# A state-space layer rebuilt around units of one state and 1024 tokens, its products shared out over four engines

## The chip, the core and the metric

The kernel runs on one core of a Trainium2 chip. A core has a matrix engine (TensorE, PE in the profile; its weight loads are listed as PEld), a vector engine (VectorE, DVE), a scalar engine for activation functions (ScalarE, ACT), a general engine (GpSimd, POOL) and a sequencer that issues most transfers (SyncE, SP). Each engine works through its own list of instructions and waits on the others by semaphores. SBUF is the on-chip memory with 128 partitions; PSUM is the smaller memory that TensorE writes. The metric is the time of one execution on the device, in microseconds. All data is fp32.

## The reference

Two layers run one after the other on x of shape (4, 512, 32, 32), each with a group norm ahead of it and a residual around it. Layer 0 is a state-space (Mamba) block on 1024 tokens per batch, 1024 inner channels and 16 states; layer 1 is an attention block with two 3x3 convolutions. The change lies in layer 0:

```python
x = features.reshape(B, C, L).transpose(0, 2, 1)
xn = (x - mu) / jnp.sqrt(var + 1e-05) * ln_w + ln_b
xz = xn @ W_in
xm, z = (xz[..., :d_inner], xz[..., d_inner:])
xc = causal depthwise convolution of xm, 4 taps
xs = jax.nn.silu((xc + conv_b[None, :, None]).transpose(0, 2, 1))
proj = xs @ W_x
dt = jax.nn.softplus(proj[..., :dt_rank] @ W_dt + b_dt)
Bm = proj[..., dt_rank:dt_rank + D_STATE]
Cm = proj[..., dt_rank + D_STATE:]
A = -jnp.exp(A_log)
def step(h, inp):
    dt_t, B_t, C_t, x_t = inp
    dA = jnp.exp(dt_t[..., None] * A)
    h = dA * h + (dt_t * x_t)[..., None] * B_t[:, None, :]
    y = jnp.einsum('bds,bs->bd', h, C_t)
    return (h, y)
y = ys.transpose(1, 0, 2) + xs * D_param
y = y * jax.nn.silu(z)
out = y @ W_out
```

(The convolution's line is written in words.) For each of 4 batches, 1024 channels and 16 states there is thus a recurrence over 1024 tokens, with one product by B ahead of it, one by C behind it, and a sum over the 16 states.

## The kernel before

Channels lie on partitions, tokens along the row. A batch of 1024 tokens is cut into two halves of T = 512, so layer 0 runs over 8 half batches (index i, `b, h = divmod(i, NH)`). The 1024 inner channels are 8 blocks of 128 (index d), and each block has 16 states (s).

For each half batch, `phase1(i)` normalizes the tokens, multiplies them by W_in (L212), convolves on VectorE (L225, L227), applies Silu (L231), and computes the parameters `proj` (L237). The rows of B and C are stored to DRAM (`bcd`), and `load_bc` loads each of the 16 pairs back, spread over all 128 partitions (`bc`, 16 buffers). `delta(i, d)` makes dt by softplus, composed of Abs, Relu, Exp and Ln, and dt times x. Then for each state, at 512 tokens:

- ScalarE: `da` = Exp(A * dt), into PSUM (L340)
- GpSimd: `dbx` = (dt x) * B (L342)
- VectorE: `ht`, the scan h = da * h + dbx, into PSUM (L344); ScalarE copies its last column for the next half (L348)
- VectorE: `hc` = ht * C (L350)
- TensorE: `hc` is added into `py` by a matmul with the identity (L351)

After 16 states VectorE adds D x (L368), and GpSimd multiplies by the gate Silu(z) (L371), whose matmul is L308. `out_proj` (L264, L270) multiplies by W_out, adds x and stores the result `x1`, which layer 1 loads.

Python generators (`phase1`, `out_proj`, `delta`) are advanced a step at a time between the states, by `drain`, so that the work of the next half batch stands among the scans of this one. The order within each engine's list is then settled by a scheduler when the program is built, from these priorities and its own estimate of times; on the chip each engine takes its list as it stands. Buffers are counted per name (`bufs`): a tile waits until the tile that last used its slot has been read for the last time. Layer 1 transforms its convolution weights first (raw loads L406, sums on VectorE and GpSimd), then goes batch by batch: `norm`, `scores`, `conv3`, `attend`, `conv3`, `finish`. Both layers use `group_stats` (L86 to L100).

## Time and profile before

Three runs took 4080.11, 4087.10 and 4087.34 us; the median is 4087.1. The profiled execution took 4090.25 us, of which the profile's span is 4088.4.

| engine | busy us | share of the span | in layer 0 (0 to 2525.6) | in layer 1 |
|---|---|---|---|---|
| TensorE | 3091.6 | 76% | 1986.4 | 1105.3 |
| VectorE | 2964.2 | 73% | 2251.9 | 712.2 |
| ScalarE | 1704.4 | 42% | 1528.3 | 176.1 |
| GpSimd | 2239.1 | 55% | 1768.4 | 470.8 |

Layer 0 ends where SP issues layer 1's first load of raw weights, at 2525.6 us. Its scans run from 96.2 to 2500.5. Layer 1 has a stretch without large matmuls, from 2525.6 to 2839, in which the weights are transformed, and then four batches. The split columns are sums over windows of the trace.

How to read the lines below: a group's line gives source line, engine, operation, output and inputs with their shapes, the count, then the busy time and the mean length of one in ns, and after the second bar the idle time of the engine just before these instructions and what ended most of it. Instructions of one engine can overlap a little, so busy time divided by count may be shorter than the mean length. A timeline's line gives the start, the length, and how many instructions of one kind it puts together.

### The profile page before, as it was taken

What the parts mean: (1) busy time and instruction counts of PE and PEld (TensorE: products, weight loads), DVE (VectorE), ACT (ScalarE), POOL (GpSimd) and SP (SyncE); (2) the same over time, 40 slices, a digit from 0 to 9 for tenths busy, and PEclk for the clock granted to TensorE, in tenths of its full rate; (3) what the DMA queues carried; (4) which work ended last, traced back from release to release, by engine and by line L of the source; (5) the groups of instructions that cost most, each with busy time, mean ns of one, the idle gap of its engine ahead of it and who ended that gap; (6) DMA issues with size and microseconds to landing.
All of it is one profiled execution on the core that took longest, in us unless ns stands there. A gap on an engine that the chain in (4) does not pass through costs nothing.

```text
span 4088.4 us, 24690 instructions
## 1 busy us (share of the span) xinstructions
PE 3091.6 (76%) x6440; PEld 1214.0 (30%) x6440; DVE 2964.2 (73%) x3429; ACT 1704.4 (42%) x2771; POOL 2239.1 (55%) x1622
## 2 busy tenths in 40 slices
PE   6776887886887886887887875002987988988988
PEld 2222332322332322332322322000433333333334
DVE  5989999889999889999889996545434534535525
ACT  3675575675575675575676562101101200200200
POOL 1767767767767767768768783666112122221222
PEclk9998999998998998999999998555898898899799
DMA  4003003003003003002002003774626527428436
GB/s 149 36 1 93 18 4 93 21 1 93 17 5 93 21 1 93 16 6 82 18 4 83 21 0 99 235 266 155 236 85 233 204 85 266 173 94 282 151 111 242
DMA packets 165013, 397.36 MB, mean 97 GB/s; under 512 B 13768, under 2 KB 81608, under 8 KB 140296
## 3 DMA queue, kind: packets, MB, share of 16 engines
q1 hardware_dynamic: 150416, 371.82, 27.1%
q10 hardware_dynamic: 14456, 23.96, 1.7%
q8 instruction: 51, 0.84, 0.1%
q14 instruction: 90, 0.74, 0.1%
HBM read 328.11 MB, written 67.63 MB: 97 GB/s over the span
## 4 chain that ended last, share of the span: by engine, by line
PE 28%; DVE 10%; POOL 9%; issue 7%; DMA 3%; ACT 2%; POOLq 0%; DVEq 0%; SPq 0%; ACTq 0%
PE m_b L613 9%; PE m_o L613 8%; PE pat L661 5%; DVE ht L344 3%; PE psc L519 2%; DVE hc L350 2%; PE py L351 2%; POOL dbx L342 2%; DMA x1t<-x 1%; PE po L264 1%; ACT da L340 1%; DVE xs L227 1%; ACT L340 1%; POOL dt L298 0%; POOL u L297 0%
## 5 line engine op out<-in xcount | busy, mean ns | idle before, releaser
L342 POOL TENSOR_TENSOR dbx<-dtx,bc 128x512 f32<-128x512 f32 x1024 | 1323.5, 1307 | 553.3 <-DVE ht L344 538.8
L351 PE MATMUL py<-hc,ident 128*128 128x512 f32 x2048 | 1126.4, 664 | 449.6 <-DVE hc L350 445.0
L340 ACT ACTIVATE da<-dt,a_sb 128x512 f32<-128x512 f32 x1024 | 699.7, 691 | 418.7 <-DVE ht L344 414.7
L351 PEld LDWEIGHTS py<-hc,ident 128*128 128x128 f32 x2048 | 365.5, 200 | 1169.4 <-DVE hc L350 1015.2
L350 DVE TENSOR_TENSOR hc<-ht,bc 128x512 f32<-128x512 f32 x1024 | 666.7, 677 | 49.2 <-ACT state L348 29.1
L344 DVE TENSOR_TENSOR_SCAN ht<-da,state,dbx 128x512 f32<-128x512 f32 x512 | 636.5, 1277 | 46.5 <-POOL dbx L342 24.1
L344 DVE TENSOR_TENSOR_SCAN ht<-da,dbx 128x512 f32<-128x512 f32 x512 | 607.8, 1218 | 65.1 <-POOL dbx L342 30.0
L613 PE MATMUL m_o<-uw_o,v_o 128*128 128x512 f32 x768 | 341.6, 607 | 56.1 <-DVE v_o L600 56.1
L613 PE MATMUL m_b<-uw_b,v_b 128*128 128x512 f32 x768 | 357.6, 624 | 5.7 <-DVE v_b L600 5.7
L264 PE MATMUL po<-xs,wpr_sb 128*128 128x512 f32 x512 | 255.7, 623 | 16.7 <-POOL xs L371 16.7
L308 PE MATMUL pz<-xt,win_sb 128*128 128x512 f32 x512 | 255.3, 613 | 14.2 <-ACT state L348 10.4
L212 PE MATMUL pxm<-xt,win_sb 128*128 128x512 f32 x512 | 248.7, 611 | 11.1 <-DVE xt L203 7.0
L98 PE MATMUL pv_l<-gdev_l,gm_sb 128*128 128x1 f32 (+1 forms) x40 | 10.9, 342 | 309.8 <-DVE gdev_l L96 309.8
L348 ACT COPY state<-ht 128x1 f32<-128x1 f32 x512 | 78.7, 157 | 379.4 <-DVE ht L344 377.6
L340 ACT ACT_TABLE_LOAD x179 | 229.7, 1283 | 3.1
L613 PEld LDWEIGHTS m_o<-uw_o,v_o 128*128 128x128 f32 x768 | 149.0, 195 | 248.4 <-issue 184.8
L661 PE MATMUL pat<-y_b,st 128*128 128x512 f32 x512 | 220.4, 592 | 0.0
L613 PEld LDWEIGHTS m_b<-uw_b,v_b 128*128 128x128 f32 x768 | 149.4, 198 | 210.8 <-issue 199.9
L227 DVE SCALAR_TENSOR_TENSOR xs<-xm,cw_sb,xs 128x512 f32<-128x512 f32 x192 | 176.0, 917 | 1.8
L667 DVE SCALAR_TENSOR_TENSOR xg<-pat,rz,xg 128x512 f32<-128x512 f32 x32 | 24.1, 752 | 195.9 <-PE pat L661 195.9
L621 ACT ACTIVATE e_o<-m_o 128x512 f32<-128x512 f32 x24 | 14.3, 597 | 336.8 <-PE m_o L613 336.8
L264 PEld LDWEIGHTS po<-xs,wpr_sb 128*128 128x128 f32 x512 | 102.2, 201 | 150.1 <-issue 123.4
(208 smaller groups left out, 3540.2 us busy)
## 6 DMA issues: line engine op xcount, KB each, us to landing
uw_b<-u_b SPq DMA_DIRECT2D x96, 1024.0 KB, 4.8
uw_o<-u_o SPq DMA_DIRECT2D x96, 1024.0 KB, 4.8
bc<-bcd SPq DMA_DIRECT2D x128, 512.0 KB, 5.4
u_b<-o_b SPq DMA_DIRECT2D x16, 768.0 KB, 5.3
u_o<-o_o SPq DMA_DIRECT2D x16, 768.0 KB, 3.8
raw_b<-in_w_bottom_dram SPq DMA_DIRECT2D x8, 1152.0 KB, 9.2
raw_o<-in_w_out_dram SPq DMA_DIRECT2D x8, 1152.0 KB, 9.2
xt<-in_x_dram SPq DMA_DIRECT2D x8, 1024.0 KB, 5.3
```

Of the source, the lines that this page charges most:

```text
L212: nc.tensor.matmul(pxm, win_sb[:, c, d * P : (d + 1) * P], t[:, c, :], start=(c == 0), stop=(c == NCC - 1),)
L227: nc.vector.scalar_tensor_tensor(u, xm[:, k : k + T], cw_sb[:, 4 * d + k : 4 * d + k + 1], u, ALU.mult, ALU.add,)
L264: nc.tensor.matmul(po, wpr_sb[:, d, c * P : (c + 1) * P], xs[i][d], start=(d == 0), stop=(d == NDC - 1),)
L308: nc.tensor.matmul(pz, win_sb[:, c, DI + d * P : DI + (d + 1) * P], xt[i][:, c, :], start=(c == 0), stop=(c == NCC - 1),)
L340: nc.scalar.activation(da, dt, AF.Exp, scale=a_sb[:, k : k + 1])
L342: nc.gpsimd.tensor_mul(dbx, dtx, bc[:, 0, :])
L344: nc.vector.tensor_tensor_scan(ht, da, dbx, 0.0 if h == 0 else state[:, k : k + 1], ALU.mult, ALU.add)
L350: nc.vector.tensor_mul(hc, ht, bc[:, 1, :])
L351: nc.tensor.matmul(py, ident, hc, start=(s == 0), stop=(s == NS - 1))
L519: nc.tensor.matmul(pt, top[:, m * P : (m + 1) * P], center[:, h * T : (h + 1) * T], start=True, stop=True,)
L613: nc.tensor.matmul(m[q], v[:, q, k, c, :], w[:, c, :], start=(c == 0), stop=(c == NCC - 1 and not extra),)
L661: nc.tensor.matmul(pt, st[m][:, 2 * P * j + h : 2 * P * (j + 1) : 2], xb[m // 2][:, m % 2, :], start=(m == 0), stop=(m == NMC - 1),)
```

## The change

Layer 0 is rewritten; layer 1 differs only in `group_stats`, which takes 1/sqrt by Ln and Exp on ScalarE (`rsqrt`) instead of Sqrt and a reciprocal on VectorE.

- A unit is now one state of one channel block over all 1024 tokens of a batch: 512 units in place of 1024 half units; the state is no longer carried over, and `state` is gone.
- The B product is made in two ways. For the nine states in `B_ON_ACT`, dt x is transposed once per block (`dtxt`, tokens on partitions), ScalarE scales eight 128x128 pieces by B's column (`sc`), and TensorE transposes them back into PSUM (`u`). For the other seven, B is loaded from DRAM over all partitions (`bbc`) and GpSimd multiplies (`dbx`); there `u` holds the Exp.
- The C product is on GpSimd for twelve states and on VectorE for the four in `C_ON_DVE`. C is loaded for every unit (`cbc`, three buffers) instead of once per half batch.
- The sum over states is made by transposes of `hc` that add up in PSUM (`y`, tokens on partitions); at the end of a block the sum is copied and transposed back (`gate`).
- W_in is scaled by ln_w, stored to DRAM (`wind`) and loaded in slices; ln_b goes into biases. The convolution reads PSUM, its first tap on ScalarE. Softplus is one activation. The gates go to DRAM (`szd`) and back, as do the gated outputs (`gd`), and W_out is loaded in slices with one buffer.
- `background` says what of the next batch stands beside which block: norms (n), convolution blocks (digits), gates (z), parameters (p).

The diff, its added lines cut to the core:

```diff
+    def rsqrt(out, var):
+        nc.scalar.activation(out, var, AF.Ln, bias=eps)
+        nc.scalar.activation(out, out, AF.Exp, scale=-0.5)
...
-        nc.scalar.activation(rstd, pv[:, :n], AF.Sqrt, bias=eps)
-        nc.vector.reciprocal(rstd, rstd)
+        rsqrt(rstd, pv[:, :n])
...
-        bp = l0.enter_context(tc.tile_pool(name="l0bc", bufs=NS))
         mmp = l0.enter_context(tc.tile_pool(name="l0mm", bufs=2, space=PSUM))
-        yp = l0.enter_context(tc.tile_pool(name="l0y", bufs=2, space=PSUM))
-        ap = l0.enter_context(tc.tile_pool(name="l0a", bufs=2, space=PSUM))
-        hp = l0.enter_context(tc.tile_pool(name="l0h", bufs=2, space=PSUM))
+        yp = l0.enter_context(tc.tile_pool(name="l0y", bufs=1, space=PSUM))
+        up = l0.enter_context(tc.tile_pool(name="l0u", bufs=2, space=PSUM))
+        NT = L // P
+        NK = T // P
+        halves = [slice(h * T, (h + 1) * T) for h in range(NH)]
+        B_ON_ACT = (0, 2, 4, 6, 8, 9, 11, 13, 15)
+        C_ON_DVE = (1, 5, 10, 14)
...
+        wind = dram.tile([2 * NDC, P, NCC, P], F32, tag="wind", name="wind")
...
+                nc.vector.tensor_scalar_mul(ws[c], ws[c], lnw_sb[:, c : c + 1])
+                nc.sync.dma_start(
+                    wind[k * NDC : (k + 1) * NDC, :, c, :].rearrange("k p n -> p k n"),
+                    ws[c].rearrange("p (k n) -> p k n", n=P),
+                )
...
+        def conv1(b, d):
+            w = load_win(b, d)
+            u = sp.tile([P, L], F32, tag="xs", name=f"xs_{b}_{d}", bufs=10)
+            hist = spool.tile([P, 3], F32, tag="hist", name=f"hist_{b}_{d}")
+            cw = [cw_sb[:, 4 * d + 3 - k : 4 * d + 4 - k] for k in range(4)]
+            for h, hs in enumerate(halves):
+                p = mmp.tile([P, T], F32, tag="mm", name=f"pxm_{b}_{d}_{h}")
+                for c in range(NCC):
+                    nc.tensor.matmul(
+                        p, w[:, c, :], xt[b][:, c, hs], start=(c == 0), stop=(c == NCC - 1)
+                    )
+                uh = u[:, hs]
+                nc.scalar.activation(uh, p, AF.Copy, scale=cw[0])
                 if h == 0:
+                    nc.scalar.copy(hist, p[:, T - 3 :])
                 for k in range(1, 4):
                     nc.vector.scalar_tensor_tensor(
+                        uh[:, k:], p[:, : T - k], cw[k], uh[:, k:], ALU.mult, ALU.add
+                    )
...
                 yield
+            nc.scalar.activation(u, u, AF.Silu, bias=cb_sb[:, d : d + 1])
+            xs[b, d] = u
...
+        def gates(b, d):
+            w = load_win(b, NDC + d)
+            sz = sp.tile([P, L], F32, tag="sz", name=f"sz_{b}_{d}", bufs=1)
+            for h, hs in enumerate(halves):
+                p = mmp.tile([P, T], F32, tag="mm", name=f"pz_{b}_{d}_{h}")
+                for c in range(NCC):
+                    nc.tensor.matmul(
+                        p, w[:, c, :], xt[b][:, c, hs], start=(c == 0), stop=(c == NCC - 1)
+                    )
+                nc.scalar.activation(
+                    sz[:, hs], p, AF.Silu, bias=bx[:, NDC + d : NDC + d + 1]
+                )
+                yield
+            nc.sync.dma_start(szd[b][d], sz)
...
+        def params(b):
+            p0 = b % 2 * NP
+            for h, hs in enumerate(halves):
+                pp = mmp.tile([P, T], F32, tag="mm", name=f"pp_{b}_{h}")
                 for d in range(NDC):
                     nc.tensor.matmul(
+                        pp[p0 : p0 + NP, :], wx_sb[:, d, :], xs[b, d][:, hs],
                         start=(d == 0), stop=(d == NDC - 1),
                     )
+                nc.scalar.copy(proj[p0 : p0 + NP, hs], pp[p0 : p0 + NP, :])
                 yield
+            nc.sync.dma_start(bcd[b], proj[p0 + RK : p0 + NP, :])
...
+            nc.vector.tensor_copy(bt_sb[b % 2], pt[:, :, RK : RK + NS])
...
+        def delta(b, d):
+            rows = slice(b % 2 * NP, b % 2 * NP + RK)
+            dt = sp.tile([P, L], F32, tag="dt", name=f"dt_{b}_{d}")
+            for h, hs in enumerate(halves):
+                pd = mmp.tile([P, T], F32, tag="mm", name=f"pd_{b}_{d}_{h}")
+                nc.tensor.matmul(
+                    pd, wdt_sb[rows, d * P : (d + 1) * P], proj[rows, hs],
+                    start=True, stop=True,
+                )
+                nc.scalar.activation(dt[:, hs], pd, AF.Softplus, bias=bdt_sb[:, d : d + 1])
+            yield
+            dtx = sp.tile([P, L], F32, tag="dtx", name=f"dtx_{b}_{d}")
+            nc.gpsimd.tensor_mul(dtx, dt, xs[b, d])
+            yield
+            dtxt = sp.tile([P, NT, P], F32, tag="dtxt", name=f"dtxt_{b}_{d}")
+            for h in range(NH):
+                pt = mmp.tile([P, NK, P], F32, tag="mm", name=f"pdt_{b}_{d}_{h}")
+                for k in range(NK):
+                    at = h * NK + k
+                    nc.tensor.transpose(pt[:, k, :], dtx[:, at * P : (at + 1) * P], ident)
+                nc.scalar.copy(dtxt[:, h * NK : (h + 1) * NK, :], pt)
+            dts[b, d] = dt, dtx, dtxt
...
+        def unit(b, d, s, y):
+            dt, dtx, dtxt = dts[b, d]
+            name = f"{b}_{d}_{s}"
+            c_bc = sp.tile([P, L], F32, tag="cbc", name=f"cbc_{name}", bufs=3)
+            nc.sync.dma_start(c_bc, bcd[b][NS + s].partition_broadcast(P))
+            u = up.tile([P, L], F32, tag="u", name=f"u_{name}")
+            scale = a_sb[:, d * NS + s : d * NS + s + 1]
+            if s in B_ON_ACT:
+                sc = sp.tile([P, NT, P], F32, tag="sc", name=f"sc_{name}")
+                for k in range(NT):
+                    nc.scalar.activation(
+                        sc[:, k, :], dtxt[:, k, :], AF.Copy,
+                        scale=bt_sb[b % 2][:, k, s : s + 1],
+                    )
+                    nc.tensor.transpose(u[:, k * P : (k + 1) * P], sc[:, k, :], ident)
+                da = sp.tile([P, L], F32, tag="da", name=f"da_{name}")
+                nc.scalar.activation(da, dt, AF.Exp, scale=scale)
+                dbx = u
+            else:
+                b_bc = sp.tile([P, L], F32, tag="bbc", name=f"bbc_{name}")
+                nc.sync.dma_start(b_bc, bcd[b][s].partition_broadcast(P))
+                dbx = sp.tile([P, L], F32, tag="dbx", name=f"dbx_{name}")
+                nc.gpsimd.tensor_mul(dbx, dtx, b_bc)
+                da = u
+                nc.scalar.activation(da, dt, AF.Exp, scale=scale)
+            hc = sp.tile([P, L], F32, tag="hc", name=f"hc_{name}", bufs=3)
+            if s in C_ON_DVE:
+                nc.vector.tensor_tensor_scan(u, da, dbx, 0.0, ALU.mult, ALU.add)
+                nc.vector.tensor_mul(hc, u, c_bc)
+            else:
+                ht = sp.tile([P, L], F32, tag="ht", name=f"ht_{name}")
+                nc.vector.tensor_tensor_scan(ht, da, dbx, 0.0, ALU.mult, ALU.add)
+                nc.gpsimd.tensor_mul(hc, ht, c_bc)
+            for k in range(NT):
+                nc.tensor.matmul(
+                    y[k // NK][:, k % NK, :], hc[:, k * P : (k + 1) * P], ident,
+                    start=(s == 0 and k % NK == 0), stop=(s == NS - 1 and k % NK == NK - 1),
+                    is_transpose=True, skip_group_check=True,
+                )
+        def gate(b, d, y):
+            sz = sp.tile([P, L], F32, tag="szl", name=f"szl_{b}_{d}", bufs=1)
+            nc.sync.dma_start(sz, szd[b][d])
+            yt = sp.tile([P, NT, P], F32, tag="yt", name=f"yt_{b}_{d}", bufs=1)
+            g = sp.tile([P, L], F32, tag="g", name=f"g_{b}_{d}", bufs=1)
+            u = xs.pop((b, d))
+            for h, hs in enumerate(halves):
+                nc.scalar.copy(yt[:, h * NK : (h + 1) * NK, :], y[h])
+            for h, hs in enumerate(halves):
+                p = mmp.tile([P, T], F32, tag="mm", name=f"pyb_{b}_{d}_{h}")
+                for k in range(NK):
+                    nc.tensor.transpose(p[:, k * P : (k + 1) * P], yt[:, h * NK + k, :], ident)
+                nc.vector.scalar_tensor_tensor(
+                    p, u[:, hs], dp_sb[:, d : d + 1], p, ALU.mult, ALU.add
+                )
+                nc.vector.tensor_mul(g[:, hs], p, sz[:, hs])
+            nc.sync.dma_start(gd[b][:, d, :], g)
+            del dts[b, d]
...
+        def out_proj(b):
+            src = x[b].rearrange("(c p) h w -> p c (h w)", p=P)
+            wsrc = w_proj.rearrange("(d p) n -> p d n", p=P)
+            for h, hs in enumerate(halves):
+                gt = sp.tile([P, NDC, T], F32, tag="gt", name=f"gt_{b}_{h}", bufs=1)
+                nc.sync.dma_start(gt, gd[b][:, :, hs])
+                for c in range(NCC):
+                    w = sp.tile([P, NDC, P], F32, tag="wpr", name=f"wpr_{b}_{h}_{c}", bufs=1)
+                    nc.sync.dma_start(w, wsrc[:, :, c * P : (c + 1) * P])
+                    res = sp.tile([P, T], F32, tag="res", name=f"res_{b}_{h}_{c}", bufs=3)
+                    nc.sync.dma_start(res, src[:, c, hs])
+                    po = mmp.tile([P, T], F32, tag="mm", name=f"po_{b}_{h}_{c}")
+                    for d in range(NDC):
+                        nc.tensor.matmul(
+                            po, w[:, d, :], gt[:, d, :], start=(d == 0), stop=(d == NDC - 1)
+                        )
+                        if d == NDC // 2 - 1:
+                            yield
+                    nc.vector.tensor_add(res, res, po)
+                    nc.sync.dma_start(x1[b][h][c * P : (c + 1) * P, :], res)
...
+        def background(b, d):
+            n = b + 1
+            if b == 0 and d < 2:
+                for k in range(4 * d, 4 * d + 4):
+                    yield from gates(b, k)
+                return
+            if n == B:
+                return
+            plan = (
+                {2: "n0", 3: "123", 4: "45z", 5: "6zz", 6: "7pz", 7: "zzzz"}
+                if b == 0
+                else {0: "n", 1: "01", 2: "23", 3: "4z", 4: "5zz", 5: "6zz", 6: "7pz", 7: "zz"}
             )
+            for what in plan.get(d, ""):
+                if what == "n":
+                    load_x(n)
+                    yield from norms(n)
+                elif what == "z":
+                    yield from gates(n, zs.pop(0))
+                elif what == "p":
+                    yield from params(n)
+                else:
+                    yield from conv1(n, int(what))
...
+        drain(norms(0))
+        for d in range(NDC):
+            drain(conv1(0, d))
+        drain(params(0))
+        drain(delta(0, 0))
+        opr = iter(())
+        for b in range(B):
+            zs = list(range(NDC))
             for d in range(NDC):
+                bg = background(b, d)
+                if d + 1 < NDC:
+                    ahead = delta(b, d + 1)
+                elif b + 1 < B:
+                    ahead = delta(b + 1, 0)
+                else:
+                    ahead = iter(())
+                y = [
+                    yp.tile([P, NK, P], F32, tag=f"y{h}", name=f"y_{b}_{d}_{h}")
+                    for h in range(NH)
+                ]
                 for s in range(NS):
+                    unit(b, d, s, y)
+                    drain(bg, 1)
+                    if d < 4 and s % 4 == 1:
+                        drain(opr, 1)
+                    if s >= 10 and s % 2 == 0:
                         drain(ahead, 1)
+                drain(bg)
                 drain(ahead)
+                gate(b, d, y)
+            opr = out_proj(b)
+        drain(opr)
```

## The prediction

> **What bounds the kernel now.** The windows come first, cut at the first scan (94.2), the end of the last scan's work (2500.5), the first load of layer 1 (2525.6) and layer 1's first large matmuls (2839). Columns: stretch, length, busy time of each engine, granted clock, DMA share, GB/s.
>
> ```profile
> 0.00:94.20 94.20, 57.73 (x117) 22.67 (x118) 47.12 (x77) 25.59 (x45) 11.14 (x22) 0.94 0.41 128
> 94.20:2500.50 2406.30, 1909.81 (x3830) 698.28 (x3828) 2201.22 (x2558) 1502.75 (x2437) 1755.97 (x1392) 0.95 0.12 36
> 2500.50:2525.60 25.10, 18.83 (x40) 7.70 (x38) 3.58 (x6) 0.00 (x0) 1.26 (x1) 0.93 0.22 73
> ```
>
> Layer 0 lasts 2525.6 us, and in its 2406.3 us of scans VectorE is busy for 2201.2, 91%. The groups say with what, and the waits that it hardly ever stands still:
>
> ```profile
> L342 POOL TENSOR_TENSOR dbx<-dtx,bc 128x512 f32<-128x512 f32 x1024 | 1323.5, 1307 | 553.3 <-DVE ht L344 538.8
> L351 PE MATMUL py<-hc,ident 128*128 128x512 f32 x2048 | 1126.4, 664 | 449.6 <-DVE hc L350 445.0
> L350 DVE TENSOR_TENSOR hc<-ht,bc 128x512 f32<-128x512 f32 x1024 | 666.7, 677 | 49.2 <-ACT state L348 29.1
> L344 DVE TENSOR_TENSOR_SCAN ht<-da,state,dbx 128x512 f32<-128x512 f32 x512 | 636.5, 1277 | 46.5 <-POOL dbx L342 24.1
> L344 DVE TENSOR_TENSOR_SCAN ht<-da,dbx 128x512 f32<-128x512 f32 x512 | 607.8, 1218 | 65.1 <-POOL dbx L342 30.0
> ```
>
> The last number before the arrow is idle time ahead of the group: 160.8 us for all scans and products together, while GpSimd, TensorE and ScalarE (414.7 at L340) each wait 400 us and more for VectorE. The others run ahead of the scan; nothing after it returns to it soon. So VectorE's work is the time: 1911 us of scans and C products.
>
> **Prices.** The timeline shows what instructions back to back take (start, length, engine, line, count):
>
> ```profile
> 399.71 2.41 DVE L344 TENSOR_TENSOR_SCAN ht<-da,state,dbx 128x512 f32<-128x512 f32 x2
> 406.57 1.26 DVE L350 TENSOR_TENSOR hc<-ht,bc 128x512 f32<-128x512 f32 x2
> 401.03 2.48 POOL L342 TENSOR_TENSOR dbx<-dtx,bc 128x512 f32<-128x512 f32 x2 [3.02 <-DVE ht L344]
> 2842.37 1.24 ACT L510 ACTIVATE top<-pt,bt_sb 64x128 f32<-64x128 f32 x4
> 4074.86 1.21 PE L685 MATMUL po<-ident,y_o 128*128 128x128 f32 x8 [1.28 <-POOL y_o L634]
> 65.95 3.70 PE L212 MATMUL pxm<-xt,win_sb 128*128 128x512 f32 x8 [0.23 <-ACT hist L223]
> ```
>
> Over 1024 tokens I take: scan 2.4, product 1.2 on VectorE and 2.5 on GpSimd, Exp 1.1 (1135 ns at L533); eight 128x128 transposes 1.1 (L685, 1.21 with the first one's latency); a 512-column matmul 0.92 (3.70 for four); a table load 1.28. A 128x128 ScalarE copy with its own scale has no row. From below it is a quarter of the 0.58 between two 512 copies, 0.15; from above the 128x128 Exp at L143, 0.31; four 128-wide copies follow each other by 0.26 at L510. I take 0.22, eight in 1.8.
>
> **The change by engine sums.** There are 512 units (4 batches, 8 channel blocks, 16 states). VectorE: 512 scans x 2.4 = 1229, 128 products x 1.2 = 154, convolution 192 x 0.62 plus corrections 140, gate 64 x 1.3 = 83, norms and output adds 90: about 1700, where it had 2250 in layer 0. GpSimd: (224 + 384) x 2.5 = 1520 plus 48 others = 1640. ScalarE: 2304 copies x 0.22 = 507, 512 Exp = 563, other 300, some 260 table loads = 333: 1700 (1540 to 1910 by the bounds). TensorE: 4096 + 2304 + 512 transposes x 0.137 = 950, and 830 matmuls x 0.92 and more = 900: 1850. By sums alone layer 0 would fall. The page "TensorE: Matmul & The Clock Gate" of the Trainium skill, section "Part 4: PE-mode transpose", speaks against it: a 128x128 transpose took about 275 ns inside a kernel there; the row above has 1.21 us for eight. By that figure the 6900 transposes would be an estimated 1900 us, not 950, and the forecast some 700 us longer; the row decides here.
>
> **What the sums leave out: who waits for whom.** In which order the instructions stand on each engine in the changed program is known before it runs. TensorE's list goes: part of u(s+2), y(s), y(s+1), rest of u(s+2), with matmuls of the next batch between them. y(s) is the transposes that add state s into the sum; it waits for the C product, mostly GpSimd's, which waits for scan s. u(s+2) is needed by scan s+2, and its slot (two in PSUM) is free only after scan s. So the scan now waits for a chain that starts at the scan before it: C product 2.5 (5 when two stand in a row), y 1.1, last u 0.3. Nothing in the trace of before has such a return. I walked the four lists by hand with the prices above and 0.1 per hand-over, first batch 3, block 5, which has no side work. Scan 1 starts at 0. Scan 2 runs 3.6 to 6.0; GpSimd's product 2 to 8.6; y2 to 9.8; the eighth transpose of u4 to 10.1; scan 4 starts at 10.2 where scan 3 ended at 8.4: 1.8 lost. In the same way scan 6 loses 1.8 (behind y4), scan 8 4.3 (y6 and y7; product 7 follows product 6 on GpSimd), scan 11 5.2 (its u stands among transposes of the next block's dt*x, which GpSimd makes after products 8, 9 and one B product), scan 13 4.3 (y11, y12), scan 15 2.4 (y13), the next scan 0 4.2 (y15). That is 24.0 lost on 16 x 2.4 + 4 x 1.2 + gate 2.6 = 45.8 of work: 69.8 us for the group; the next scan 1 waits for y15, the copy of y, its transposes back and the gate.
>
> Side work makes it longer, since matmuls stand ahead of u on TensorE. In batch 1, block 2 (two convolutions, two output blocks, 32 matmuls) u2 comes after 12 matmuls and y1, and scan 2 starts at 14.9 instead of 3.6; I reach 92, with 56 of VectorE work. Batch 1, block 5 (24 matmuls) gives 85; batch 3, block 1 (16) gives 73. The slope from 70 is 0.2 to 0.7 us a matmul; I take 0.6. Convolutions, gates, output, norms and parameters put 192 + 256 + 192 + 48 + 48 = 736 matmuls beside the 32 groups. Groups: 32 x 70 + 736 x 0.6 = 2240 + 440 = 2680, 84 each.
>
> **The ends of layer 0.** Nothing covers them. Before the first scan everything is now done for 1024 tokens: eight convolution blocks at 7.4 (two times 3.70) instead of 4.2, +26; the parameter matmuls +7; the second half's norm (3.7 + 2.5 + 3.8, Ln and Exp with two table loads 3.8) +14; GpSimd's four products 10 instead of 5; more tables, weights scaled and sent through DRAM, transposes, +15. From 96 this makes 165 (140 to 190). After the last scan: gate 9; g stored and 2 MB of it loaded twice, 11 each (2 MB landed in 11.4 at start); eight blocks of 7.4 on TensorE, each behind a 512 KB slice of w_proj in its only buffer (5.4 to landing by the bc loads), the first slice loaded early, 97: 128 (95 to 150) where 25 was. SP issues layer 1's first load behind all of these stores, so layer 1 moves with them. The new group_stats takes Ln and Exp for a root and a reciprocal: 16 times in layer 1 up to 2.8 more, some hidden by loads: +15 (0 to 45). Conv edges, folded bias and ln weights are in the walked lists.
>
> **Sum.** 165 + 2680 + 128 = 2973 against 2525.6: +447; layer 1 +15. The profiled execution took 4090.25 (span 4088.4), 3.1 above the median of 4087.1: 4090 + 462 = 4552, told as 4550. Break-even is (2525.6 - 293 - 15) / 32 = 69.3 us a group: even the group without side work lies there.
>
> **Bounds.** GpSimd's 1024 product is 2.35 by L634 (the shortest 128x1024 sum) and 2.84 by L640; eight transposes are 1.0 or, by the last twelve of L685 in 2.79, 1.9. That makes the bare group 68 to 79; with a slope of 0.2 to 0.8 the groups are 2320 to 3120, and the time, with the ends' bounds, 4130 to 5070. SP's new loads (736 broadcasts of 512 KB, 377 MB, 140 GB/s over the groups) stand in three and two buffers; the 16 such loads around 380 us ran at 300 GB/s and landed in 5.4, a product uses its own three units (12 us) after its slot frees, so I cost them at nothing, up to 5 us a group where szl or gd stands before them.
>
> **Rivals.** (a) The waits matter less than walked: the scheduler's lists meet another rhythm, u is done early, and a group follows the engine sums plus some 10 us, 60 to 64 in the mean. Then 293 + 32 x 62 = 2277, and the time is 3860. For it: four nearly equal sums of 50 to 58 a group. Against: y before u in the lists, and no slack in two slots. It decides where a group's mean falls under 69.3. (b) ScalarE or the loads add to the chain: table loads (15 of them, 19 us, in the block with four gates) and copies at 0.31 put it beyond 66 in gate and norm blocks, or C broadcasts come late: 8 to 12 more a group, 4870. For it: Silu, Exp and Softplus alternate in the list; against: ScalarE's Exp and copies mostly stand ahead of their use in my walks.
>
> **How the numbers follow.** Forecast 0.65, (b) 0.20, (a) 0.13, and 0.02 around no change. The slower cases reach from 4130 to 5070; I cut both outer edges and take 4220 to 4870, which leaves out (a) and the top of (b). Faster 0.12, within 0.2% 0.01 (about what a measurement of this kernel can tell), slower 0.87.
>
> **What would show it.** Right: first scan near 165; VectorE near 60% in layer 0; groups of 70 to 75 us in batch 3 and 85 to 95 before; the largest waits TensorE's y for GpSimd's C product and VectorE's scan for TensorE's u; layer 1's first load near 2970; layer 1 itself nearly unchanged. Wrong: VectorE, GpSimd or TensorE above 85% in the scans, a group mean under 70, or scans that wait for loads.

## The result and the profile after

The changed kernel takes 4685.3 us (median of four runs, 4682.98 to 4688.07); the kernel before, on the same chip, 4086.8 us (four runs, 4080.11 to 4087.34). The ratio is 1.147, with a 95% interval of 1.145 to 1.149: 15% slower. The forecast was 4550 us, in a range of 4220 to 4870. The profiled execution took 4686.39 us, with a span of 4684.6.

The windows of the changed kernel, cut at its first scan, the end of its last scan, and layer 1's first load (columns as before: stretch, length, busy time of TensorE, weight loads, VectorE, ScalarE, GpSimd, granted clock, DMA share, GB/s):

```profile
0.00:167.30 167.30, 129.40 (x359) 69.15 (x360) 56.74 (x127) 55.33 (x81) 14.62 (x12) 0.96 0.33 104
167.30:2974.07 2806.77, 1978.51 (x8506) 1344.53 (x8504) 1564.12 (x1106) 1800.37 (x3459) 1513.50 (x649) 0.80 0.53 176
2974.07:3111.88 137.81, 80.28 (x144) 34.28 (x144) 8.35 (x13) 2.43 (x4) 2.34 (x1) 0.70 0.28 88
3111.88:4684.50 1572.62, 1106.68 (x2456) 486.56 (x2456) 707.53 (x772) 208.87 (x328) 471.69 (x208) 0.80 0.54 188
```

The second line is the case. In 2806.8 us of scans VectorE is busy for 1564.1 (56%; it was 91%), TensorE for 70%, ScalarE for 64%, GpSimd for 54%. VectorE has less to do, no engine took its place as the bound, and the stretch became 400 us longer. Where the engines stand still is in the groups (busy time and mean length in ns of one, then idle time ahead and what ended it):

```profile
L379 POOL TENSOR_TENSOR hc<-ht,cbc 128x1024 f32<-128x1024 f32 x384 | 898.6, 2350 | 1130.4 <-DVE ht L378 1082.5 <-issue 42.2 <-PE u L361 3.9
L381 PE MATMUL y<-ident,hc 128*128 128x128 f32 x4096 | 771.8, 352 | 646.3 <-POOL hc L379 615.9 <-DVE hc L375 29.7
L357 ACT ACTIVATE sc<-dtxt,bt_sb 128x128 f32<-128x128 f32 x2304 | 712.3, 389 | 38.1 <-PE u L361 38.0
L378 DVE TENSOR_TENSOR_SCAN ht<-da,u 128x1024 f32<-128x1024 f32 x288 | 656.1, 2284 | 1027.8 <-PE u L361 861.8 <-ACT sc L357 74.1 <-POOL dbx L369 49.4
L361 PE MATMUL u<-ident,sc 128*128 128x128 f32 x2304 | 436.7, 322 | 161.2 <-DVE ht L378 90.6 <-ACT sc L357 66.8 <-ACT da L363 3.7
```

The waits form a ring. GpSimd's C product waits 1082.5 us for the scan, TensorE's y waits 615.9 for the C product, and the scan waits 861.8 for TensorE's u. Before, the idle time on the scans' lines was 46.5 and 65.1. No engine of the ring is busy for more than some 70% of the stretch; each waits for another. The link that closes the ring is the order of TensorE's list, which these sums don't show as a wait: u itself waits only 161.2 us, because it stands behind y. Scan 8 of the block below shows it: GpSimd's two C products end at 2797.80, y runs from 2797.86, the last two transposes of u follow at 2799.62, and the scan starts at 2800.39.

The same can be seen state by state. VectorE's timeline for batch 3, block 5, which has no work beside it (start, length, idle before and its releaser; only the gates at both ends and the scans that waited are shown):

```profile
2769.02 1.39 DVE L400 SCALAR_TENSOR_TENSOR pyb<-xs,dp_sb,pyb 128x512 f32<-128x512 f32 x2
...
2777.39 2.29 DVE L378 TENSOR_TENSOR_SCAN ht<-da,u 128x1024 f32<-128x1024 f32 x1 [2.33 <-PE u L361]
2784.18 2.29 DVE L378 TENSOR_TENSOR_SCAN ht<-da,u 128x1024 f32<-128x1024 f32 x1 [2.32 <-PE u L361]
2790.76 2.29 DVE L378 TENSOR_TENSOR_SCAN ht<-da,u 128x1024 f32<-128x1024 f32 x1 [0.85 <-PE u L361]
2800.39 4.46 DVE L378 TENSOR_TENSOR_SCAN ht<-da,u 128x1024 f32<-128x1024 f32 x2 [5.16 <-PE u L361]
2813.11 2.29 DVE L378 TENSOR_TENSOR_SCAN ht<-da,u 128x1024 f32<-128x1024 f32 x1 [4.81 <-ACT sc L357]
2821.96 2.29 DVE L378 TENSOR_TENSOR_SCAN ht<-da,u 128x1024 f32<-128x1024 f32 x1 [4.38 <-PE u L361]
2831.97 2.29 DVE L378 TENSOR_TENSOR_SCAN ht<-da,u 128x1024 f32<-128x1024 f32 x1 [4.27 <-PE u L361]
2839.04 2.29 DVE L378 TENSOR_TENSOR_SCAN ht<-da,u 128x1024 f32<-128x1024 f32 x1 [4.79 <-PE u L361]
2841.24 1.39 DVE L400 SCALAR_TENSOR_TENSOR pyb<-xs,dp_sb,pyb 128x512 f32<-128x512 f32 x2
```

From gate to gate the block takes 72.2 us. The scans shown are those of states 2, 4, 6, 8, 11, 13, 15 and of the next state 0: all the scans whose B product goes through TensorE, except scan 9, which follows scan 8 at once. Their idle times add up to 28.9. (Scan 11, the line with ScalarE's sc, started just after the last transpose of its u had ended, at 2812.97; the first five of the eight had run at 2810.81, and the other three stood among transposes of the next block's dt times x, which GpSimd finished at 2812.05.) The scans whose B product is GpSimd's (1, 3, 5, 7, 10, 12, 14) are not late.

Block times by batch, from the first L400 instruction of one block's end to that of the next, averaged over a batch's eight blocks: 93.4, 92.7, 91.7 and 73.8 us. Batch 3's blocks 4 to 7, with nothing beside them, took 72.5, 72.2, 73.7 and 64.6.

### The profile page after: what moved, and what is told of

It is laid out like the page before. It is cut to its first block, busy times and chain, and to the rows that moved or that the text cites. A ratio compares the mean times of both kernels' runs of the same rounds, so it can differ in the third digit from the quotient of the medians.

```text
span 4684.6 us, 34360 instructions
## 1 busy us (share of the span) xinstructions
PE 3294.9 (70%) x11464; PEld 1934.5 (41%) x11464; DVE 2336.7 (50%) x2018; ACT 2067.0 (44%) x3871; POOL 2002.1 (43%) x870
## 5 line engine op out<-in xcount | busy, mean ns | idle before, releaser
L379 POOL TENSOR_TENSOR hc<-ht,cbc 128x1024 f32<-128x1024 f32 x384 | 898.6, 2350 | 1130.4 <-DVE ht L378 1082.5
L381 PE MATMUL y<-ident,hc 128*128 128x128 f32 x4096 | 771.8, 352 | 646.3 <-POOL hc L379 615.9
L378 DVE TENSOR_TENSOR_SCAN ht<-da,u 128x1024 f32<-128x1024 f32 x288 | 656.1, 2284 | 1027.8 <-PE u L361 861.8
L381 PEld LDWEIGHTS y<-ident,hc 128*128 128x128 f32 x4096 | 636.2, 183 | 866.2 <-POOL hc L379 774.8
L357 ACT ACTIVATE sc<-dtxt,bt_sb 128x128 f32<-128x128 f32 x2304 | 712.3, 389 | 38.1 <-PE u L361 38.0
L369 POOL TENSOR_TENSOR dbx<-dtx,bbc 128x1024 f32<-128x1024 f32 x224 | 527.5, 2357 | 161.0 <-DMA bbc<-bcd 65.8
L361 PE MATMUL u<-ident,sc 128*128 128x128 f32 x2304 | 436.7, 322 | 161.2 <-DVE ht L378 90.6
L361 PEld LDWEIGHTS u<-ident,sc 128*128 128x128 f32 x2304 | 340.0, 170 | 276.9 <-ACT sc L357 172.3
L729 PE MATMUL m_b<-uw_b,v_b 128*128 128x512 f32 x768 | 358.7, 626 | 10.4 <-DVE v_b L716 10.4
L363 ACT ACTIVATE da<-dt,a_sb 128x1024 f32<-128x1024 f32 x288 | 328.2, 1140 | 0.9
L374 DVE TENSOR_TENSOR_SCAN u<-u,dbx 128x1024 f32<-128x1024 f32 x128 | 292.0, 2281 | 25.7 <-POOL dbx L369 14.3
```

The costliest lines, as they stand in the source:

```text
L357: nc.scalar.activation(sc[:, k, :], dtxt[:, k, :], AF.Copy, scale=bt_sb[b % 2][:, k, s : s + 1],)
L361: nc.tensor.transpose(u[:, k * P : (k + 1) * P], sc[:, k, :], ident)
L363: nc.scalar.activation(da, dt, AF.Exp, scale=scale)
L369: nc.gpsimd.tensor_mul(dbx, dtx, b_bc)
L374: nc.vector.tensor_tensor_scan(u, da, dbx, 0.0, ALU.mult, ALU.add)
L378: nc.vector.tensor_tensor_scan(ht, da, dbx, 0.0, ALU.mult, ALU.add)
```

## The experiments

All runs are of the changed kernel with the edit whose core is shown, unless it is said otherwise; a time without a range is that of a single run; line numbers in a run's profile shift with its edit. Their block times are taken as above.

### y behind u: same work, another order on TensorE

```diff
-                    unit(b, d, s, y)
+                    held.append((s, unit(b, d, s, y)))   # returns hc
+                    if len(held) > 2:
+                        with tc.issue_after(last_u[0].ins):
+                            add_y(y, *held.pop(0))        # the eight transposes of L381
```

> The changed kernel with one difference: TensorE's list. The transposes that add state s into the sum (y) are given out two units later and stand behind the last transpose of u(s+2), so that u(s+2) no longer stands behind y(s), which waits for the C product of s. All engines do the same work, hc keeps three buffers, u two. Theory (the return chain scan, C product, y, u, scan through TensorE's list costs the time): the walk of batch 3, block 5 by the new list loses some 14 us instead of 24, most of it at u11 and at the block's end; 58 to 62 us where 72 were measured, groups of the other batches near 72 instead of 92, so layer 0 near 2520 and the time 4000 to 4250. Rival (ScalarE's copies, table loads, or the slower TensorE set the time, the order of y only fills what is left): the engines' work is the same, the groups stay within 4 us of 88, time above 4550. Rival (loads of C come late): the same, above 4550.

It took 4232.75 us (4226.05 to 4243.08; ratio to before 1.035, 1.033 to 1.036): 452.6 less than the changed kernel, three quarters of the loss, for an order alone. Batch means are 78.0, 77.0, 76.5 and 64.7 us, the block looked at 60.6: the block as walked, the other batches some 5 us over what was expected. Its windows' second line, and the group of its scans:

```profile
167.33:2532.89 2365.56, 1830.41 (x8506) 1234.88 (x8504) 1590.44 (x1106) 1779.19 (x3449) 1513.86 (x649) 0.86 0.61 209
```

```profile
L382 DVE TENSOR_TENSOR_SCAN ht<-da,u 128x1024 f32<-128x1024 f32 x288 | 656.1, 2281 | 550.2 <-PE u L363 308.8 <-ACT da L367 116.9 <-ACT yt L403 78.9
```

The counts and busy times of VectorE, ScalarE and GpSimd are nearly the same (1590, 1779, 1514 us against 1564, 1800, 1514). What went is the wait for u: 308.8 us instead of 861.8. (TensorE's instructions are the same ones too, but its busy time fell from 1978.5 to 1830.4 us as its granted clock rose from 0.80 to 0.86; how much of the gain is this was not parted.) The scans' stretch became 441 us shorter, more than the 400 it had grown; what is left of the loss stands at the ends of layer 0 (71 us more than before ahead of the first scan, 109 after the last) and, with 10, in layer 1. So the return through TensorE's list is shown, and the sums are not what held the changed kernel.

### y behind u, and y waits for nothing

```diff
-                    y[k // NK][:, k % NK, :], hc[:, k * P : (k + 1) * P], ident,
+                    y[k // NK][:, k % NK, :], dts[b, d][1][:, k * P : (k + 1) * P], ident,
```

> As the kernel with y behind u, and in addition y transposes dt*x of the block in place of the C product hc, so that y waits for nothing; hc is still computed. The sum over states is therefore not the reference's. It shows what is left when no instruction of TensorE waits for a C product. Theory: groups follow the engine sums plus the block's end and u11, 52 to 60 us in batch 3, 60 to 68 in the mean, time 3850 to 4100. If ScalarE sets the time: groups stay above 80 and ScalarE is busy over 85% in the scans, time above 4450.

4029.7 us; batch means 72.3, 69.0, 69.2 and 59.3. With no C product in the ring at all, the scans' stretch is 2157 us, 67.4 a block. The sum over the states is not the reference's here: y adds up dt times x. The time is what the work would take in this order of instructions if y were free of its wait, and it is only 1.5% under the kernel before: the ends of layer 0 (below) take the rest.

### C loaded once per block

```diff
-            c_bc = sp.tile([P, L], F32, tag="cbc", name=f"cbc_{name}", bufs=3)
-            nc.sync.dma_start(c_bc, bcd[b][NS + s].partition_broadcast(P))
+            if s == 0:
+                cbs[0] = sp.tile([P, L], F32, tag="cbc", name=f"cbc_{name}", bufs=3)
+                nc.sync.dma_start(cbs[0], bcd[b][NS + s].partition_broadcast(P))
+            c_bc = cbs[0]
```

> The changed kernel, with C loaded once per block (the row of state 0) instead of once per unit, 480 broadcasts of 512 KB fewer; the C product is therefore not the reference's. The lists of the engines stay nearly as they were. Theory (return chain): the loads are hidden, time 4640 to 4700, the same within 1%. Rival (C's broadcasts come late, or the transfers slow others): 5 us a group or more, time below 4530.

4706.6 us, 0.5% over the changed kernel and just above the expected 4640 to 4700. The windows' second line of this run:

```profile
165.88:2997.63 2831.75, 1996.19 (x8506) 1356.20 (x8504) 1564.35 (x1106) 1802.96 (x3461) 1511.95 (x648) 0.79 0.25 85
```

The traffic fell from 176 to 85 GB/s, and the stretch did not get shorter. In the changed kernel C's loads are hidden; that costing them at nothing was right is shown. The loads of B stayed as they were; GpSimd's B products waited 65.8 us for them in the changed kernel.

### One scaled copy in place of eight

```diff
-                for k in range(NT):
-                    nc.scalar.activation(
-                        sc[:, k, :], dtxt[:, k, :], AF.Copy,
-                        scale=bt_sb[b % 2][:, k, s : s + 1],
-                    )
-                    nc.tensor.transpose(u[:, k * P : (k + 1) * P], sc[:, k, :], ident)
+                nc.scalar.activation(
+                    sc, dtxt, AF.Copy, scale=bt_sb[b % 2][:, 0, s : s + 1]
+                )
+                for k in range(NT):
+                    nc.tensor.transpose(u[:, k * P : (k + 1) * P], sc[:, k, :], ident)
```

> The changed kernel, with the eight scaled ScalarE copies of a unit (sc) replaced by one over all 1024 columns, scaled by one column of B; the B product is therefore not the reference's. ScalarE's work falls by about 72 x 0.309 - 9 x 1.1 = 12 us a block of 16 states, TensorE keeps its transposes. Theory (return chain): u waits for its slot and for y in TensorE's list, not for the copies; the groups change by 0 to -4 us, time 4560 to 4690. Rival (ScalarE's copies bound or lengthen the chain): the groups fall by 8 to 12 us, time 4300 to 4430.

4396.0 us: 289 less, as the rival had it (4300 to 4430) and not as the theory had it (4560 to 4690). The group of the scans in this run:

```profile
L377 DVE TENSOR_TENSOR_SCAN ht<-da,u 128x1024 f32<-128x1024 f32 x288 | 654.5, 2281 | 677.6 <-PE u L360 645.0 <-POOL hc L378 10.8 <-POOL dbx L368 10.2
```

The scans' wait for u was 861.8 us, here it is 645.0. All idle time ahead of the scans (this line and the two of the other scans) fell from 1063.8 to 775.7, 288 less, which is the whole gain. The copies lie inside the ring: u cannot be transposed before sc is scaled; u's transposes waited 66.8 us for sc, here 10.4. But the edit moved more than ScalarE. The scheduler also made dt times x of the next block earlier, so that its transposes no longer stand among those of u11.

To part the two, the same copy was put into the kernel with y behind u.

> y behind u, and the eight scaled copies of a unit replaced by one over 1024 columns (the B product is not the reference's). ScalarE's work falls by some 12 us a block; TensorE's list has y and u as in the kernel with y behind u, but dt*x of the next block is made earlier on GpSimd and its transposes no longer stand among those of u11. If the time that one copy alone saved (some 290 us) was ScalarE's own work, it is saved here too: 3940 to 4060. If it was the return chain in another guise (u11 and the y before it), which y behind u has mostly taken away, this run comes within 70 of the 4233 of y behind u, 4160 to 4260.

4138.3 us, 94 under y behind u. Neither figure that was expected: two thirds of what one copy had saved is gone once y stands behind u, one third stays. The copies and the order of y work on the same wait. How much of the 289 us is ScalarE's time and how much is the shifted lists was not parted further and stays open.

### The transposes of the next block behind u13

```diff
+                with tc.issue_after(last_u[0].ins) if last_u else nullcontext():
                     for k in range(NK):
                         at = h * NK + k
                         nc.tensor.transpose(pt[:, k, :], dtx[:, at * P : (at + 1) * P], ident)
```

> y behind u, and the eight transposes of the next block's dt*x (pdt), which stood among the transposes of u11 and made them wait for GpSimd's dt*x, are given out behind the last transpose of u13. Nothing is left out. In the profile of y behind u scan 11 of batch 3, block 5 lost 7.65 us to this u11. Theory (TensorE's list holds the scans by what stands ahead of u): scan 11 loses under 2 us, a block gains 4 to 6 us, of which the next scan 0 may give back 1, time 4060 to 4140. Rival (ScalarE is next in line; sums decide): the loss moves to the scan after it, time within 30 of 4233.

4217.7 us (4207.16 to 4225.47): 15 less than y behind u, where the theory had 90 to 170 less. The rival was right. VectorE's timeline of batch 3, block 5 with y behind u, the scans of states 11, 13, 15 and the next 0:

```profile
2404.84 2.29 DVE L382 TENSOR_TENSOR_SCAN ht<-da,u 128x1024 f32<-128x1024 f32 x1 [7.65 <-PE u L363]
2409.59 2.29 DVE L382 TENSOR_TENSOR_SCAN ht<-da,u 128x1024 f32<-128x1024 f32 x1 [0.29 <-POOL hc L383]
2415.75 2.29 DVE L382 TENSOR_TENSOR_SCAN ht<-da,u 128x1024 f32<-128x1024 f32 x1 [0.36 <-ACT sc L359]
2423.20 2.29 DVE L382 TENSOR_TENSOR_SCAN ht<-da,u 128x1024 f32<-128x1024 f32 x1 [5.16 <-PE u L363]
```

and the same four with the next block's transposes behind u13:

```profile
2367.51 2.29 DVE L381 TENSOR_TENSOR_SCAN ht<-da,u 128x1024 f32<-128x1024 f32 x1 [2.58 <-ACT da L366]
2374.79 2.29 DVE L381 TENSOR_TENSOR_SCAN ht<-da,u 128x1024 f32<-128x1024 f32 x1 [2.81 <-POOL hc L382]
2384.36 2.29 DVE L381 TENSOR_TENSOR_SCAN ht<-da,u 128x1024 f32<-128x1024 f32 x1 [3.78 <-ACT sc L358]
2391.44 2.29 DVE L381 TENSOR_TENSOR_SCAN ht<-da,u 128x1024 f32<-128x1024 f32 x1 [4.79 <-PE u L362]
```

Scan 11 gains 5.1 us, about as walked (2.58 is left, where under 2 was expected), and scans 13 and 15 lose 2.5 and 3.4, by their releasers to GpSimd and ScalarE: 13.5 us of idle time before, 14.0 after. Once y stands behind u, several engines are late by nearly the same amount, and mending one shows the next.

### y one unit later still

```diff
-                    if len(held) > 2:
+                    if len(held) > 3:
-            hc = sp.tile([P, L], F32, tag="hc", name=f"hc_{name}", bufs=3)
+            hc = sp.tile([P, L], F32, tag="hc", name=f"hc_{name}", bufs=4)
```

(On top of the run before, and two buffers instead of three for the W_in slices and `res`.)

> y one unit later still: y(s) is given out with unit s+3, behind the last transpose of u up to u(s+3), with four buffers of hc; to make room for them the slices of W_in and the tile res have two buffers instead of three. The transposes of the next block's dt*x stand behind u13, as in the run before. Nothing is left out. Theory (what is left over 4030, the time with a y that waits for nothing, is y's wait for the C product ahead of u): most of the 200 us between y behind u and that run is got back, time 4060 to 4150. Rival (with y behind u the rest is spread over ScalarE's copies, GpSimd's products and the block's end, and the loss only moves): within 30 of 4218.

4161.1 us (4159.1 to 4168.24; ratio to before 1.019, 1.017 to 1.022): 57 less, between the two expectations. It is the fastest of the runs that compute everything and keep the nine units on ScalarE and TensorE, and still slower than the kernel before. TensorE's weight loads for u now wait 293.7 us for ScalarE's copies, where they waited 165.2 with y behind u. But the run whose y waits for nothing has 261.5 of this wait too, so it does not account for the 131 us left to that run. What does was not parted; still there are 145.0 us of y's wait for GpSimd's C product, and 98.4 us of scans that wait, by their releaser, for the copy of y at a block's end.

### All B products on GpSimd

No unit's B product passes TensorE, so there is no u behind a y; C is on VectorE for eleven states.

```diff
-        B_ON_ACT = (0, 2, 4, 6, 8, 9, 11, 13, 15)
+        B_ON_ACT = ()
-        C_ON_DVE = (1, 5, 10, 14)
+        C_ON_DVE = (0, 1, 3, 4, 6, 7, 9, 10, 12, 13, 15)
```

(Without the transposed dt times x; four buffers each for `bbc` and `cbc`.)

> No unit's B product goes through TensorE: all 16 on GpSimd, C on VectorE for eleven states, on GpSimd for states 2, 5, 8, 11, 14; the transposed dt*x is not made; four buffers each for the broadcasts of B and C. Nothing is left out. There is no u to wait for behind a y. Sums a block: VectorE 16 x 2.28 + 11 x 1.22 + 2.6 = 52.5, and 10 of convolution; GpSimd 21 x 2.35 + 2.4 = 52. Theory: VectorE is the bound again, idle ahead of scans under 5 us a block, groups of 62 to 68, time 3850 to 4050. Rival (loads: 32 broadcasts of 512 KB a block, 260 GB/s): scans wait for B products that wait for transfers, groups above 70, time above 4100.

4599.1 us (4595.22 to 4601.91; ratio 1.125, 1.123 to 1.127): expected were 3850 to 4050. The theory that only the way through TensorE is at fault falls. The time lies where the rival, the loads, had it (above 4100), and B products did wait 309.1 us for loads over the run; but scans waited 633.4 us for B products on their largest line, and only 23.2 of the 309.1 fall in the 309 us from 2580 on, where the blocks still take over 76. GpSimd and VectorE in the timeline of batch 3 (VectorE's products left out):

```profile
2621.46 2.34 POOL L372 TENSOR_TENSOR hc<-ht,cbc 128x1024 f32<-128x1024 f32 x1 [4.73 <-PE y L374]
2623.76 7.11 POOL L362 TENSOR_TENSOR dbx<-dtx,bbc 128x1024 f32<-128x1024 f32 x3
...
2626.14 2.30 DVE L367 TENSOR_TENSOR_SCAN u<-u,dbx 128x1024 f32<-128x1024 f32 x1 [4.81 <-POOL dbx L362]
2629.67 2.29 DVE L367 TENSOR_TENSOR_SCAN u<-u,dbx 128x1024 f32<-128x1024 f32 x1
2633.19 2.28 DVE L371 TENSOR_TENSOR_SCAN ht<-u,dbx 128x1024 f32<-128x1024 f32 x1
2635.60 2.34 POOL L372 TENSOR_TENSOR hc<-ht,cbc 128x1024 f32<-128x1024 f32 x1 [4.74 <-PE y L374]
2637.90 7.12 POOL L362 TENSOR_TENSOR dbx<-dtx,bbc 128x1024 f32<-128x1024 f32 x3
...
2640.29 2.30 DVE L367 TENSOR_TENSOR_SCAN u<-u,dbx 128x1024 f32<-128x1024 f32 x1 [4.82 <-POOL dbx L362]
```

It is the same ring with one engine fewer. GpSimd's list has a C product, then three B products. The C product at 2635.60 starts just after the scan at 2633.19 ends, at 2635.5. (The releaser named is TensorE's y, but the y that frees the third buffer of hc was done at 2625.8; the scan came last.) The next B product stands behind it, and the scan at 2640.29 waits for that. One turn is a B product of 2.35, three scans and two VectorE products of together 9.3, and a C product of 2.35: 14.0 us for three states (the two B waits stand 14.15 apart), 75 for sixteen; batch 3's last blocks took 76.4 to 78.1.

### Four units through TensorE, twelve B products on GpSimd

```diff
-        B_ON_ACT = (0, 2, 4, 6, 8, 9, 11, 13, 15)
-        C_ON_DVE = (1, 5, 10, 14)
+        B_ON_ACT = (0, 4, 8, 12)
+        C_ON_DVE = (1, 3, 5, 7, 9, 11, 13, 15)
```

(On top of y behind u.)

> y behind u, B products by ScalarE and TensorE for states 0, 4, 8, 12 only (nine before), on GpSimd for the other twelve; C products on VectorE for the odd states, on GpSimd for the even ones. Nothing is left out. Sums a block: VectorE 16 x 2.28 + 8 x 1.22 + gate 2.6 = 49, and 10 of convolution; GpSimd 20 x 2.35 + 2.4 = 49; ScalarE 32 x 0.31 + 16 x 1.1 + 10 = 38. Theory (the units were never too much work, the return through TensorE was): with five fewer units on the path through TensorE the groups come to 60 to 66 us, time 3800 to 3990, faster than the kernel before. If GpSimd's products in a row hold the scans instead, groups of 72 and more and 4180 and more.

4362.4 us (4356.43 to 4364.58; ratio 1.068, 1.065 to 1.070), 130 slower than y behind u with nine units. Scans wait 386.1 us for GpSimd's B products (282.2 and 103.9 on their two lines) and still 209.7 for u; the B products wait 336.1 us for B's loads. The time lies where the rival had it, and its groups (77.8 in the mean, 72 and more were named) too; but the rival named GpSimd's products in a row, and a good part of their lateness is the loads'.

### B products ahead of the C product on GpSimd

B products all on GpSimd with four buffers; C on GpSimd for states 2, 6 and 10 only, three units later:

```diff
+            if held and s == held[0][0] + 3:
+                at, name, ht, c_bc = held.pop(0)
+                with tc.issue_after(last[0].ins):      # the B product of s + 3
+                    nc.gpsimd.tensor_mul(hc, ht, c_bc)
-        w = sp.tile([P, NDC, P], F32, tag="wpr", name=f"wpr_{b}_{h}_{c}", bufs=1)
+        w = sp.tile([P, NDC, P], F32, tag="wpr", name=f"wpr_{b}_{h}_{c}", bufs=2)
```

> As the kernel with all B products on GpSimd, with three differences: dbx has four buffers instead of two; C is on GpSimd for states 2, 6, 10 only, and GpSimd gets that product three units later, behind the B product of s+3, so that GpSimd does not wait for scan s with the next B products behind it; w_proj slices have two buffers. Nothing is left out. VectorE a block: 16 x 2.28 + 13 x 1.22 + 2.6 = 55, and some 11 of convolution and norms in batches 0 to 2. Theory (B products all on GpSimd made a second return chain, scan, C product, B product, scan, in GpSimd's list): with it gone VectorE is the bound, groups 57 to 60 in batch 3 and 64 to 70 before it; the stretch after the last scan falls from 138 to 100 to 120; time 3840 to 4010, faster than the kernel before. Rival (loads or shared memory ports slow the products): products or scans longer than 2.4 us, or scans that wait for products that wait for loads, 4100 and more.

4318.5 us (4313.74 to 4324.53; ratio 1.058, 1.056 to 1.060), where the theory had 3840 to 4010. GpSimd's wait for the scan is no longer among its waits, and another is there: 759.6 us of B products that wait for B's loads, as the rival had it. Its other half, slower products, is not seen: a product took 2.35 us on GpSimd and a scan 2.29, as in the other runs. The second run of the pair has all C products on VectorE, the division of the kernel before:

> All B products on GpSimd with four buffers for dbx, and all C products on VectorE: the kernel before's division of work at 1024 tokens a unit, with no way back from a scan to GpSimd but through the buffers of dbx. Nothing is left out. VectorE a block: 16 x (2.28 + 1.22) + 2.6 = 58.6, and 11 beside it in batches 0 to 2. Theory: groups of 60 to 62 in batch 3, 69 to 72 before, time 3980 to 4090. Rival (loads): 4150 and more.

4268.6 us, also in the rival's range. Blocks 4 to 7 of batch 3 took 62.1, 62.4, 61.1 and 60.6 us, as worked out; the blocks with work beside them 68 to 100 in batches 1 and 2, where 69 to 72 were expected. The wait, in the list of waits of this run (total, times, longest):

```profile
POOL dbx L362 <- DMA bbc<-bcd: 906.7, 361, 14.3
```

and how it comes about, in its timeline:

```profile
2313.51 1.23 DVE L368 TENSOR_TENSOR hc<-u,cbc 128x1024 f32<-128x1024 f32 x1 [0.44 <-DVE u L367]
...
2314.77 0.32 SPq L344 DMA_DIRECT2D cbc<-bcd  x1
2315.18 0.38 SPq L360 DMA_DIRECT2D bbc<-bcd  x1
...
2321.20 2.35 POOL L362 TENSOR_TENSOR dbx<-dtx,bbc 128x1024 f32<-128x1024 f32 x1 [0.96 <-DMA bbc<-bcd]
```

A third ring, in SP's list. The load of C for a coming unit waits for a C product to free its buffer (2314.74), the load of B stands behind it (2315.18) though its own buffer was free from 2310.7, lands 6 us later, and the B product waits for it. How much of the 906.7 us is this order and how much is the rate of the transfers (269 GB/s in this run's stretch, 176 in the changed kernel's) was not parted. Here the loads, which the changed kernel hides, are on the path.

The stretch after the last scan shows the last two lines of the edit by themselves, in the first run of the pair, which has them:

```profile
2649.33:2741.74 92.41, 63.85 (x144) 28.94 (x144) 9.57 (x15) 2.43 (x4) 0.00 (x0) 0.81 0.40 129
```

With a second buffer for the slices of W_out the stretch is 92.4 us; in the runs with one it is 133 to 138.

### The new root alone, in the kernel before

```diff
-        nc.scalar.activation(rstd, pv[:, :n], AF.Sqrt, bias=eps)
-        nc.vector.reciprocal(rstd, rstd)
+        nc.scalar.activation(rstd, pv[:, :n], AF.Ln, bias=eps)
+        nc.scalar.activation(rstd, rstd, AF.Exp, scale=-0.5)
```

> The kernel before with one line of the change: the root of a group's variance by Ln and Exp on ScalarE instead of Sqrt and a reciprocal on VectorE. Layer 1 (from its first load to the end) took 1562.8 us before and 1572.7 after. If these 9.9 us are the new root: layer 1 takes 1569 to 1576 here. If they come from somewhere else (where layer 1 finds the queues and the clock): 1560 to 1566.

4111.2 us. Layer 1 took 1568.6 us (span 4109.5, first load at 2540.9): 5.8 more than before, between the two expectations. Layer 1 has the same code in the changed kernel and in the other runs above, and took 1568.4 to 1576.4 us there. So neither the 5.8 us nor the 4 that are left of the 9.9 is clear of the spread: that the new root costs layer 1 something fits the runs, how much stays open. In layer 0 the first load came 15.3 us later, in this one run; the seven runs of the kernel before beside it lie within 15 us of one another, so that figure is uncertain too.

## Why the prediction was right, and where it was off

The likeliest case happened, by its mechanism and in its place. One thing in the sum is luck: losses that were told too small stand against work that was told too large. Step by step:

- **First scan.** 165 forecast (its terms, added to 96, give 163), 167.3 measured. The prediction's windows begin with the first scan at 94.2; in the trace of before it starts at 96.2, which is what the sum went by.
- **The walk.** For batch 3, block 5: losses of 1.8, 1.8, 4.3, 5.2, 4.3, 2.4 and 4.2 us at scans 4, 6, 8, 11, 13, 15 and the next 0. Measured: 2.3, 0.9, 5.2, 4.8, 4.4, 4.3 and 4.8, and 2.3 at scan 2, which the walk did not have. 28.9 us instead of 24.0. The work came out smaller: 43.3 instead of 45.8, since a scan took 2.29 and not 2.4. In all 72.2 us instead of 69.8.
- **Groups.** Batch 3 was told as 70 to 75, the others as 85 to 95; they took 64.6 to 78.8 and 84.5 to 97.9. The mean is 87.7 and not 84: 32 bare blocks at some 72.8 (blocks 4 to 6 of batch 3) instead of 70 make 90 us, and the rest, 477 us for 736 matmuls beside them, is 0.65 each instead of 0.6, another 37.
- **After the last scan.** 128 forecast, 137.8 measured, and bound as worked out by the one buffer of W_out slices (the second buffer took off 41 us from 133).
- **Layer 1.** 15 forecast, 9.9 measured.
- **Sum.** 4552 was too short by 134: 127 in the groups, 2 and 10 at the ends, 5 back in layer 1. So layer 1's first load came at 3111.9 and not near 2970, and VectorE was busy for 52% of layer 0 (56% of the scans' stretch) where near 60% was told. The largest waits are the two that were named, and with them GpSimd's for the scan.

**The terms that were mis-sized** are two prices that were taken too low. The scaled copy of 128x128 on ScalarE was taken at 0.22 us; it took 0.309 (712.3 / 2304), the upper bound that the working named, and 2.43 for eight instead of 1.8. Eight transposes were taken at 1.1; on average y took 1.51 (771.8 / 4096 each). GpSimd's product, 2.35 instead of 2.5, and the scan went the other way. By engine, layer 0's sums were 1629, 1530, 1858 and 2188 us for VectorE, GpSimd, ScalarE and TensorE, against some 1700, 1640, 1700 and 1850.

**The step that failed** is a clause among the rivals: that ScalarE's copies "mostly stand ahead of their use in my walks". One copy in place of eight saved 289 us, all of it in the scans' waits, and 94 with y behind u. So the copies were part of the ring; but the order of other transposes moved in the same edit, and what the copies alone cost stays open. Rival (b) named this cost, and that part of its mechanism was at work inside the forecast's; its other part, late loads of C, was not. Rival (a), that the waits matter less, would have needed blocks under 69.3 us. They came near that only where y stood behind u (73.9, and 71.2 with y one unit later still; 70.6 with one copy) and were under it only where y waited for nothing (67.4).

**The rule on transposes.** The page "TensorE: Matmul & The Clock Gate" of the Trainium skill, section "Part 4: PE-mode transpose", gives about 275 ns for one inside a kernel, beside a figure for bf16; the forecast went by 0.137 us from the row of eight in 1.21. Busy time over count, by which TensorE's sum goes, is 0.188 for y and 0.190 for u: between the two. (The lengths of single ones, which overlap, are 352 and 322 ns in the groups' lines.) For 6900 transposes that is an added 350 us of TensorE's time over the forecast, not the 950 that the page's figure would have added.

**What the change bought.** The run with the kernel before's division of work shows what the new form is worth without the ring through TensorE: its scans' stretch is 2399.5 us, as long as that of the kernel before (2403.1, from the first scan at 96.2 to the end of the last at 2499.3), with 140 us less of VectorE's work in it (2059.9 against 2200.0) and more waits. Its distance, 178 us in the spans, is at layer 0's ends: 67 ahead of the first scan, 107 after the last, 7 in layer 1, less the 4. No run that computes everything beat the kernel before.

## What to carry to other kernels

When a product is shared out over engines, follow the ring and not the sums: write down for one unit who waits for whom, in the order in which each list holds them, and look for a place where work for a later unit stands behind work that waits for an earlier one. Such a ring costs its whole round trip per turn, on TensorE, on GpSimd or in a load queue, and no engine need look busy. Issuing the late consumer behind the next producer is the cheap cure (here 453 us). That more buffers alone do not cure it while the list stays the same follows from the lists; no run here tested it.
